# Level 2 cross attention: scores with the keys on the partitions, maxima found and spread by two transpositions

## The chip, the cores and the metric

The kernel runs on one core of one Trainium2 chip. The time is that of the device, in microseconds (us), from start to end of one execution; a median of several executions is given where there are several. Everything is computed in fp32.

## The reference, cut to what matters

The reference is a four-level perceiver: each level is a cross attention to a long context, an attention-like mixing of the latent rows, and a feed-forward part. The changed part is the cross attention of level 2. It has 2 batches of 64 latent rows with 256 features, 2 batches of 1024 context rows with 192 features, and 16 heads of 64 features.

```python
def _L2_xattn_ref(x, context, w_q, w_k, w_v, w_o, b_o):
    ...
    q = (x @ w_q).reshape(B, Sq, HEADS, DIM_HEAD).transpose(0, 2, 1, 3)
    k = (context @ w_k).reshape(B, Skv, HEADS, DIM_HEAD).transpose(0, 2, 1, 3)
    v = (context @ w_v).reshape(B, Skv, HEADS, DIM_HEAD).transpose(0, 2, 1, 3)
    sim = jnp.einsum('bhid,bhjd->bhij', q, k) * SCALE
    attn = jax.nn.softmax(sim, axis=-1)
    out = jnp.einsum('bhij,bhjd->bhid', attn, v)
    out = out.transpose(0, 2, 1, 3).reshape(B, Sq, INNER)
    return out @ w_o + b_o
...
x = x + _L2_xattn_ref(_layernorm(x, axis=-1), ctx_768, ...)
```

No mask is applied in this part.

## The kernel before

All 128 latent rows (2 batches of 64) lie on the 128 partitions, and the program goes through the levels one after the other, stage by stage. Each stage opens its own pools of SBUF tiles. Two pools lie in PSUM: `two_banks()` gives a tile of 1024 columns over two banks, `bank()` one of 512; in this stage there are two of the first kind and four of the second, and a tile is given again when its last reader is done. `weight(name)` takes a tile from a ring of weight tiles and issues its load on the SP queue. `stat()` gives a small tile from a ring.

The cross attention of level 2 (L1545 to L1656) never forms keys or values. The query of each head is multiplied with the head's key weights instead, so that scores are products of a 192-wide query with the raw context; the output is the weighted sum of raw context rows, multiplied with the head's value weights afterwards.

1. L1555 to L1564: layernorm of x, its transposition, and the queries of all heads, `qT`, scaled by 0.125. Around it run the last steps of `kv3.values`, work for level 3 that fills waits of PE.
2. L1569 to L1585: queries through the key weights, to `qA` (the first 128 of 192 context features) and `qB` (the other 64, kept twice, once on each half of the partitions), in four groups of eight matmuls; each group fills a `two_banks()` tile and is evicted by `evacuate`, which alternates between VectorE and ScalarE.
3. L1595 to L1651: the loop over 16 units, a unit being a pair of heads `j` and a batch `b`. A unit has 128 queries (2 heads x 64 rows) and 1024 keys. Scores have the queries on the partitions and the keys on the columns: `qA` is the stationary operand and the turned context `ctxA` (128 features) streams by in two pieces of 512 keys (L1601); the 64 remaining features, `ctxB`, are added by two matmuls on the two halves of the array (L1606). VectorE takes the maximum of each query over its 1024 keys (L1611), ScalarE the exponential with the negated maximum as its bias, and the sum of the row with it (L1613).
4. The second part of a unit, `finish`, runs one unit later (`later`, L299): p is turned in eight pieces of 128x128 (`transposed`, L244; PE at L251, copies at L102 and L104), the turned pieces weigh the context rows `crows` (`accumulate`, L261, eight matmuls of 192 columns), and VectorE divides by the row's sum, giving `u` (L1624).
5. The third part, `project`, runs one unit later still: `u` is turned (L1629), copied by ScalarE to `uT` (L1632), and for every second unit multiplied with the value weights (L1641) and copied to `oT` (L1647).
6. L1654 to L1656: the product with `wo` and the residual. The sum of x and the bias is done on GpSimd (`residual`, L263).

An fp32 matmul shows in the profile as two records, each with its weight load, and a transposition as one. Only the layernorm part of the stage stands in `in_written_order` (L273), which ties each instruction of PE, VectorE, ScalarE and GpSimd to the one written before it on the same engine; the order of the rest is found by the scheduler of the language, which is free to bring later scores ahead of weighing.

The context rows `crows` are loaded at L1550 with one DMA of 12288 contiguous bytes per partition. On the SP queue it stands between the loads of level 2's next stage (`l2t_qkv` ahead of it, `l2t_gate`, `l2t_val`, `l2t_proj` behind it).

## Time and profile before

| | |
|---|---|
| median of 3 runs | 725.84 us (725.58 to 725.9) |
| profiled execution: its own time | 727.3 us |
| profiled execution: span of the records | 725.6 us |
| mean granted TensorE clock | 0.976 |
| PE busy, share of the span | 670.8 us, 92% |
| VectorE (DVE) busy | 286.9 us, 40% |
| ScalarE (ACT) busy | 266.6 us, 37% |
| GpSimd (POOL) busy | 65.9 us, 9% |
| level 2 cross attention: first scores to the first matmul with `wo` | 284.72 to 398.45 |

PE is TensorE's matmuls, PEld its weight loads, which overlap them. Times inside the profile are us from the start of the span; "L261" is a line of the kernel file, and a line can be that of a helper (all accumulated matmuls of the program have L261). A row of the timeline gives the start, the length, the engine, the line, the operation, what it writes and reads, and, in brackets, how long the engine sat idle before it and what ended that. A row of the groups gives the busy time of all instructions of one line and form and the mean length of one in nanoseconds. The lengths of matmuls are modelled, and overlapping ones are counted once.

### The profile page before, as it was taken

To read this page: it belongs to the slowest core of one execution; us is meant where nothing else is said; L and a number is where in the kernel's file an instruction comes from. 1 tells how busy PE (TensorE), PEld (TensorE's weight loads), DVE (VectorE), ACT (ScalarE), POOL (GpSimd) and SP (SyncE) were. 2 spreads that over 40 slices of the span, in tenths; PEclk is the share of its full clock that TensorE was granted. 3 is DMA by queue.
4 is the path that set the end of the run, shared out by engine and by line. 5 is a ranking of instruction groups with operands and counts; after the bars stand their busy time and mean duration, and the time that the engine had idled before them with its cause. 6 is when DMAs were issued, how large, how long until landed. Compare 5 with 4: busy or idle time off the path is not lost.

```text
span 725.6 us, 11293 instructions
## 1 busy us (share of the span) xinstructions
PE 670.8 (92%) x4628; PEld 493.7 (68%) x4628; DVE 286.9 (40%) x724; ACT 266.6 (37%) x540; POOL 65.9 (9%) x92
## 2 busy tenths in 40 slices
PE   7799979989989999999999989999999989779997
PEld 3456657946659996767766678999979856543543
DVE  5844443157550003343333335525331267533111
ACT  2353252258643333333323324405231278432111
POOL 3520100000100000000000030130000000000340
PEclk9899999989999999999999999999999999969999
DMA  8940012840007886000000400011138800447981
GB/s 283 412 175 1 1 50 92 291 170 1 3 1 255 305 282 261 1 0 1 1 1 1 174 1 1 1 63 55 59 132 312 304 8 2 157 206 296 361 328 66
DMA packets 19302, 92.76 MB, mean 128 GB/s; under 512 B 3042, under 2 KB 5620, under 8 KB 10324
## 3 DMA queue, kind: packets, MB, share of 16 engines
q1 hardware_dynamic: 16976, 85.70, 31.8%
q0 software_dynamic: 2016, 6.30, 2.3%
q8 instruction: 36, 0.59, 0.3%
q14 instruction: 14, 0.11, 0.0%
q10 hardware_dynamic: 260, 0.06, 0.0%
HBM read 98.20 MB, written 0.13 MB: 136 GB/s over the span
## 4 chain that ended last, share of the span: by engine, by line
PE 85%; DVE 8%; ACT 5%; issue 2%; DMA 0%; POOL 0%; DVEq 0%; ACTq 0%; POOLq 0%
PE bank L261 34%; PE two_banks L590 5%; PE two_banks L1601 4%; PE bank L1343 4%; PE bank L251 3%; PE two_banks L1314 3%; PE bank L635 2%; PE two_banks L1606 2%; PE two_banks L379 2%; PE bank L1369 2%; PE two_banks L1773 2%; PE bank L1893 2%; PE two_banks L405 1%; PE two_banks L381 1%; PE two_banks L261 1%
## 5 line engine op out<-in xcount | busy, mean ns | idle before, releaser
L261 PEld LDWEIGHTS bank<-l2x_ctx,pT 128*128 128x128 f32 x256 | 42.3, 190 | 7.8 <-ACT pT L104 4.7
L261 PE MATMUL bank<-l2x_ctx,pT 128*128 128x192 f32 x256 | 44.4, 327 | 0.6 <-ACT pT L104 0.6
L354 DVE SCALAR_TENSOR_TENSOR x_new<-bank,comb,x_new 128x256 f32<-128x256 f32 x24 | 11.6, 484 | 80.0 <-PE bank L261 80.0
L1343 PEld LDWEIGHTS bank<-ident,p 128*128 128x128 f32 x256 | 29.9, 150 | 18.1 <-issue 6.5
L1343 PE MATMUL bank<-ident,p 128*128 128x128 f32 x256 | 39.8, 300 | 1.3 <-ACT pT L1352 0.5
L1322 DVE TENSOR_REDUCE negmax<-two_banks 128x1 f32<-128x1024 f32 x32 | 37.6, 1216 | 7.0 <-PE two_banks L1314 7.0
L1328 ACT ACTIVATE p<-two_banks,negmax 128x1024 f32<-128x1024 f32 x32 | 36.0, 1126 | 0.8 <-DVE negmax L1322 0.8
L1601 PE MATMUL two_banks<-ctxA,l2x_qA 128*128 128x512 f32 x64 | 32.6, 597 | 0.5 <-DVE l2x_qA L102 0.5
L1352 ACT COPY pT<-bank 128x512 f32<-128x512 f32 x48 | 27.0, 588 | 14.4 <-PE bank L1343 14.3
L1532 ACT ACTIVATE l1f_hT<-bank,cols 128x128 f32<-128x128 f32 x64 | 18.2, 368 | 32.9 <-PE bank L261 32.9
L261 PEld LDWEIGHTS bank<-xT,l1f_w_sb 128*128 128x128 f32 x256 | 29.7, 192 | 0.6 <-issue 0.3
L261 PE MATMUL bank<-xT,l1f_w_sb 128*128 128x128 f32 x256 | 30.1, 276 | 0.0
L261 PEld LDWEIGHTS bank<-xT,l2f_w_sb 128*128 128x128 f32 x256 | 29.6, 192 | 0.3
L261 PE MATMUL bank<-xT,l2f_w_sb 128*128 128x128 f32 x256 | 29.8, 276 | 0.0
L104 ACT COPY pT<-bank 128x512 f32<-128x512 f32 (+1 forms) x22 | 12.1, 556 | 47.6 <-PE bank L251 47.6
L261 PE MATMUL bank<-l1f_w_sb,l1f_hT 128*128 128x256 f32 x128 | 28.8, 380 | 0.0
L1611 DVE TENSOR_REDUCE negmax<-two_banks 128x1 f32<-128x1024 f32 x16 | 19.6, 1225 | 20.8 <-PE two_banks L1606 20.8
L1314 PE MATMUL two_banks<-n_kT,n_qx 32*128 32x512 f32 x128 | 24.7, 667 | 2.8 <-ACT n_kT L450 1.8
L251 PEld LDWEIGHTS bank<-ident,p 128*128 128x128 f32 x164 | 17.7, 141 | 13.8 <-issue 11.8
L261 PEld LDWEIGHTS bank<-l1f_w_sb,l1f_hT 128*128 128x128 f32 x128 | 23.8, 190 | 2.9
L268 POOL TENSOR_TENSOR x_bias<-x_new,rows 128x256 f32<-128x256 f32 x4 | 2.9, 725 | 235.1 <-DVE x_new L354 230.6
L590 PE MATMUL two_banks<-l3f_w_sb,m_xg 128*64 128x512 f32 (+1 forms) x112 | 23.4, 636 | 0.5 <-ACT m_xg L613 0.5
(558 smaller groups left out, 1313.8 us busy)
## 6 DMA issues: line engine op xcount, KB each, us to landing
l1f_w_sb<-in_l1f_w_dram SPq DMA_DIRECT2D x16, 1024.0 KB, 4.9
l3f_w_sb<-in_l3f_w_dram SPq DMA_DIRECT2D x12, 1024.0 KB, 7.5
more_w<-in_l3f_w_dram SPq DMA_DIRECT2D x12, 1024.0 KB, 11.5
l0f_w_sb<-in_l0f_w_dram SPq DMA_DIRECT2D x8, 1024.0 KB, 9.1
l2f_w_sb<-in_l2f_w_dram SPq DMA_DIRECT2D x8, 1024.0 KB, 4.7
l2f_w_sb<-in_l2f_w_dram SPq DMA_DIRECT2D x8, 512.0 KB, 4.5
xh<-in_ctx_dram SPq DMA_DIRECT2D x8, 192.0 KB, 5.8
l2x_ctx<-in_ctx_dram SPq DMA_DIRECT2D x1, 1536.0 KB
```

The lines of the kernel that those rows point to most:

```text
L251: nc.tensor.transpose(ps[:, c * P : (c + 1) * P], src[:, (at + c) * P : (at + c + 1) * P], ident)
L261: nc.tensor.matmul(dst, lhsT, rhs, start=(k == 0), stop=(k == len(pairs) - 1))
L379: nc.tensor.matmul(dst[n], ctxA[:, b, n, keys], w[:, 0, :], start=True, stop=False)
L590: nc.tensor.matmul(part[s], xg[r][:, c, s], shelf.at[r, j, n](c, f), start=False, stop=(c == 1), skip_group_check=True,)
L1314: nc.tensor.matmul(sc[u][:, n * 512 : (n + 1) * 512], qx[rows_, c, n, b].rearrange("p h q -> p (h q)"), kT[c, b][rows_, n, :], start=True, ...
L1322: nc.vector.tensor_reduce(sc[u][1], sc[u][0], AX.X, ALU.max, negate=True)
L1328: nc.scalar.activation(p[u], sc[u][0], AF.Exp, bias=sc[u][1], scale=1.0, accum_out=total[u // 4][:, u % 4 : u % 4 + 1],)
L1343: nc.tensor.transpose(ps[:, kc * P : (kc + 1) * P], p[u][:, (4 * k + kc) * P : (4 * k + kc + 1) * P], ident,)
L1352: nc.scalar.copy(dst, ps)
L1532: nc.scalar.activation(hT[:, at + f, :], ps[:, f * P : (f + 1) * P], AF.Gelu, bias=col("l1f_b1", e * 8 + at + f), scale=1.0,)
L1601: nc.tensor.matmul(dst[n], qA[:, j, b].rearrange("p h q -> p (h q)"), ctxA[:, b, n, :], start=True, stop=False,)
L1611: nc.vector.tensor_reduce(negmax, sc, AX.X, ALU.max, negate=True)
```

## The change

Scores now have the keys on the partitions: for each of eight blocks of 128 keys, the context block is the stationary operand and the unit's 128 queries stream by. The weights p come out turned as weighing needs them, so p is not transposed any more. The maximum of a query now lies across partitions. It is found in two steps: VectorE takes the maximum over the eight blocks (`largest`, a view with a step of 128 elements), PE turns the resulting 128x128 tile (`turn_largest`), VectorE takes the maximum over its columns, negated (`largest_of_all`), and a second transposition, of that column broadcast to 128 columns, spreads the values over the partitions (`spread`), with a copy to SBUF by ScalarE. VectorE then adds the negated maximum to the scores on their way from PSUM to SBUF (`shift`, two halves), and ScalarE takes the exponential in place (`exponentials`, two halves). `crows` gets a 193rd column of ones, so that weighing also yields the sum of the weights. The whole stage stands in `in_written_order`, with an order written out in the loop at its end. The queries are evicted by halves on both engines, `through_keys` uses two single banks where it used a tile of two banks, and its last call is moved behind the first scores. The tiles for attention have two buffers where they had three.

```diff
@@ -1542,115 +1542,179 @@
 
 
 
+
+
     with psum(2, 4), stage_pool(name="l2x", bufs=1) as pool, stage_pool(
-        name="l2x_att", bufs=3
-    ) as att:
+        name="l2x_att", bufs=2
+    ) as att, in_written_order():
         wq, wk, wv, wo = (weight(f"l2x_w{n}") for n in "qkvo")
-        crows = pool.tile([P, 16, CD], F32, name="l2x_ctx")
-        nc.sync.dma_start(crows, i["ctx"])
-        with in_written_order():
-
-            last = kv3.values(1, 2)
-            steps(last, 2)
-            xlT = turned_rows(layernorm(x, then=AF.Exp))
-            steps(last)
+
+        crows = pool.tile([P, 16, CD + 1], F32, name="l2x_ctx")
+        nc.sync.dma_start(crows[:, :, :CD], i["ctx"])
+        nc.gpsimd.memset(crows[:, :, CD:], 1.0)
         qT = pool.tile([P, 8, P], F32, name="l2x_qT")
-        for at in (0, 4):
+
+
+        qA = pool.tile([P, 8, NB, 2, S], F32, name="l2x_qA")
+        qB = pool.tile([P, 8, NB, 2, S], F32, name="l2x_qB")
+        oT = pool.tile([P, 8, P], F32, name="l2x_oT")
+        units = [(j, b) for j in range(8) for b in range(NB)]
+        sc, mx, turned_mx, shifts, p, po, u, uT = {}, {}, {}, {}, {}, {}, {}, {}
+
+        def queries(at):
             ps = features(xlT, wq, at, 4)
             dst = qT[:, at : at + 4, :].rearrange("p c t -> p (c t)")
-            if at == 0:
-                nc.vector.tensor_scalar(dst, ps, 0.125, None, ALU.mult)
-            else:
-                nc.scalar.activation(dst, ps, AF.Copy, scale=0.125)
-
-
-        qA = pool.tile([P, 8, NB, 2, S], F32, name="l2x_qA")
-        qB = pool.tile([P, 8, NB, 2, S], F32, name="l2x_qB")
-        for at in (0, 4):
-            for part, qc in enumerate((qA, qB)):
-                ps = two_banks()
-                for j in range(4):
-                    for h in range(2):
-                        nc.tensor.matmul(
-                            ps[:, h * 512 + j * P : h * 512 + (j + 1) * P],
-                            wk[half[h], at + j, part * P : (part + 1) * P],
-                            qT[half[h], at + j, :], start=True, stop=True,
-                        )
+            nc.vector.tensor_scalar(dst[:, :D], ps[:, :D], 0.125, None, ALU.mult)
+            nc.scalar.activation(dst[:, D:], ps[:, D:], AF.Copy, scale=0.125)
+
+        def through_keys(at, part):
+            ps = [bank(), bank()]
+            for j in range(4):
                 for h in range(2):
-                    evacuate(
-                        qc[:, at : at + 4, :, h, :],
-                        ps[:, h * 512 : (h + 1) * 512].rearrange(
-                            "p (j b q) -> p j b q", j=4, b=NB
-                        ),
+                    nc.tensor.matmul(
+                        ps[h][:, j * P : (j + 1) * P],
+                        wk[half[h], at + j, part * P : (part + 1) * P],
+                        qT[half[h], at + j, :], start=True, stop=True,
                     )
-        oT = pool.tile([P, 8, P], F32, name="l2x_oT")
-        outer = []
-
-        def last_part(work=None):
-            if outer:
-                outer.pop()()
-            if work is not None:
-                outer.append(work)
-
-        for j in range(8):
-            uT = att.tile([CH, 2, 2, NB, S], F32, name="l2x_uT", bufs=2)
-            for b in range(NB):
-                sc = two_banks()
-                dst = [sc[:, n * 512 : (n + 1) * 512] for n in range(2)]
+            for h, copy in enumerate((nc.vector.tensor_copy, nc.scalar.copy)):
+                copy(
+                    (qB if part else qA)[:, at : at + 4, :, h, :],
+                    ps[h].rearrange("p (j b q) -> p j b q", j=4, b=NB),
+                )
+
+        def scores(k):
+
+            j, b = units[k]
+            sc[k] = two_banks().rearrange("p (n t q) -> p n t q", n=2, t=4)
+            for n in range(2):
+                for t in range(4):
+                    nc.tensor.matmul(
+                        sc[k][:, n, t, :], ctxA[:, b, n, t * P : (t + 1) * P],
+                        qA[:, j, b].rearrange("p h q -> p (h q)"),
+                        start=(t == 0), stop=False, skip_group_check=True,
+                    )
+            for t in range(4):
                 for n in range(2):
                     nc.tensor.matmul(
-                        dst[n], qA[:, j, b].rearrange("p h q -> p (h q)"), ctxA[:, b, n, :],
-                        start=True, stop=False,
+                        sc[k][:, n, t, :], ctxB[half[n], b, t * P : (t + 1) * P],
+                        qB[half[n], j, b].rearrange("p h q -> p (h q)"),
+                        start=False, stop=True, skip_group_check=True,
                     )
-                for n in range(2):
+
+        def largest(k):
+            mx[k] = att.tile([P, P], F32, tag="mx", name="l2x_mx")
+            nc.vector.tensor_reduce(
+                mx[k], sc[k].rearrange("p n t q -> p q (n t)"), AX.X, ALU.max
+            )
+
+        def turn_largest(k):
+            turned_mx[k] = bank()
+            nc.tensor.transpose(turned_mx[k][:, :P], mx[k], ident)
+
+        def largest_of_all(k):
+            mx[k] = stat(name="negmax")
+            nc.vector.tensor_reduce(mx[k], turned_mx[k][:, :P], AX.X, ALU.max, negate=True)
+
+        def spread(k):
+
+            ps = turned_mx[k][:, P : 2 * P]
+            nc.tensor.transpose(ps, mx[k].to_broadcast([P, P]), ident)
+            shifts[k] = att.tile([P, P], F32, tag="shift", name="l2x_shift")
+            nc.scalar.copy(shifts[k], ps)
+
+        def shift(k):
+            p[k] = att.tile([P, 2, 4, P], F32, tag="p", name="p")
+            for n in range(2):
+                nc.vector.tensor_tensor(
+                    p[k][:, n], sc[k][:, n], shifts[k].unsqueeze(1).to_broadcast([P, 4, P]),
+                    ALU.add,
+                )
+
+        def exponentials(k):
+            for n in range(2):
+                nc.scalar.activation(p[k][:, n], p[k][:, n], AF.Exp)
+
+        def weigh(k, kcs):
+            _, b = units[k]
+            if kcs[0] == 0:
+                po[k] = bank()
+            for kc in kcs:
+                nc.tensor.matmul(
+                    po[k][:, : CD + 1], p[k][:, kc // 4, kc % 4, :], crows[:, b * 8 + kc, :],
+                    start=(kc == 0), stop=(kc == 7),
+                )
+
+        def take_u(k):
+            rinv = stat(name="rinv")
+            nc.vector.reciprocal(rinv, po[k][:, CD : CD + 1])
+            u[k] = att.tile([P, CD], F32, tag="u", name="l2x_u")
+            nc.vector.tensor_scalar(u[k], po[k][:, :CD], rinv, None, ALU.mult)
+
+        def turn_u(k):
+            j, b = units[k]
+            if b == 0:
+                uT[j] = att.tile([CH, 2, 2, NB, S], F32, tag="uT", name="l2x_uT")
+            ps = bank()
+            for c in range(2):
+                nc.tensor.transpose(
+                    ps[0:CH, c * P : (c + 1) * P], u[k][:, c * CH : (c + 1) * CH], ident
+                )
+            nc.scalar.copy(
+                uT[j][:, :, :, b, :],
+                ps[0:CH, : 2 * P].rearrange("p (c h q) -> p c h q", c=2, h=2),
+            )
+
+        def project(k):
+            j, b = units[k]
+            if b == 0:
+                return
+            ps = bank()
+            for c in range(2):
+                for h in range(2):
                     nc.tensor.matmul(
-                        dst[n], qB[half[n], j, b].rearrange("p h q -> p (h q)"),
-                        ctxB[half[n], b, :], start=False, stop=True,
+                        ps[half[h], :P],
+                        wv[:, c, (2 * j + h) * 64 : (2 * j + h + 1) * 64],
+                        uT[j][:, c, h].rearrange("p b q -> p (b q)"),
+                        start=(c == 0), stop=(c == 1),
                     )
-                negmax, total = stat(name="negmax"), stat(name="total")
-                nc.vector.tensor_reduce(negmax, sc, AX.X, ALU.max, negate=True)
-                p = att.tile([P, NK], F32, tag="p", name="p")
-                nc.scalar.activation(p, sc, AF.Exp, bias=negmax, scale=1.0, accum_out=total)
-                rinv = stat(name="rinv")
-                nc.vector.reciprocal(rinv, total)
-
-                def finish(j=j, b=b, p=p, rinv=rinv, uT=uT):
-                    pT = transposed(p, 8, att, "pT", "pT")
-                    po = bank()
-                    accumulate(
-                        po[:, :CD], [(pT[:, kc, :], crows[:, b * 8 + kc, :]) for kc in range(8)]
-                    )
-                    u = att.tile([P, CD], F32, name="l2x_u")
-                    nc.vector.tensor_scalar(u, po[:, :CD], rinv, None, ALU.mult)
-
-                    def project():
-                        ps = bank()
-                        for k in range(2):
-                            nc.tensor.transpose(
-                                ps[0:CH, k * P : (k + 1) * P], u[:, k * CH : (k + 1) * CH], ident
-                            )
-                        nc.scalar.copy(
-                            uT[:, :, :, b, :],
-                            ps[0:CH, : 2 * P].rearrange("p (k h q) -> p k h q", k=2, h=2),
-                        )
-                        if b == 0:
-                            return
-                        ps = bank()
-                        for k in range(2):
-                            for h in range(2):
-                                nc.tensor.matmul(
-                                    ps[half[h], :P],
-                                    wv[:, k, (2 * j + h) * 64 : (2 * j + h + 1) * 64],
-                                    uT[:, k, h].rearrange("p b q -> p (b q)"),
-                                    start=(k == 0), stop=(k == 1),
-                                )
-                        nc.vector.tensor_copy(oT[:, j, :], ps[:, :P])
-
-                    last_part(project)
-
-                later(finish)
-        later()
-        last_part()
+            nc.vector.tensor_copy(oT[:, j, :], ps[:, :P])
+
+
+        last = kv3.values(1, 2)
+        steps(last, 2)
+        xlT = turned_rows(layernorm(x, then=AF.Exp))
+        steps(last)
+        queries(0)
+        queries(4)
+        through_keys(0, 0)
+        through_keys(0, 1)
+        through_keys(4, 0)
+        for k in range(-1, 16):
+            if k < 15:
+                scores(k + 1)
+                largest(k + 1)
+            if k > 0:
+                turn_u(k - 1)
+            if k >= 0:
+                weigh(k, range(0, 4))
+            else:
+                through_keys(4, 1)
+            if k < 15:
+                turn_largest(k + 1)
+                largest_of_all(k + 1)
+            if k >= 0:
+                weigh(k, range(4, 6))
+            if k < 15:
+                spread(k + 1)
+                shift(k + 1)
+                exponentials(k + 1)
+            if k >= 0:
+                weigh(k, range(6, 8))
+                take_u(k)
+            if k > 0:
+                project(k - 1)
+        turn_u(15)
+        project(15)
         ps = bank()
         accumulate(ps[:, :D], [(oT[:, k, :], wo[:, k, :]) for k in range(8)])
         x = residual(x, ps[:, :D], row("l2x_bo"))
```

## Prediction

> **What bounds the kernel now.** I read the page first, then the windows of the stage, then the timeline of one unit, then the groups for single durations. The page's first part and two windows (columns: length, then busy time and count of PE, PEld, DVE, ACT, POOL, then the granted clock, the DMA share and GB/s):
>
> ```profile
> PE 670.8 (92%) x4628; PEld 493.7 (68%) x4628; DVE 286.9 (40%) x724; ACT 266.6 (37%) x540; POOL 65.9 (9%) x92
> ...
> 305.00:385.00 80.00, 80.00 (x443) 56.17 (x442) 29.33 (x54) 25.00 (x47) 0.25 (x1) 1.00 0.00 1
> 385.00:398.00 13.00, 11.21 (x70) 8.34 (x70) 3.88 (x8) 3.96 (x9) 0.57 (x4) 1.00 0.00 0
> ```
>
> In the body of this stage PE is never idle, at full clock and with nothing on the DMA engines; DVE and ACT work about a third of the time. So here time is the sum of what PE streams, and only PE's list of work counts, until some wait opens a hole in it. One unit (head pair j, batch b) in the timeline (start, length, engine, line):
>
> ```profile
> 342.96 0.38 PE L1629 MATMUL bank<-ident,l2x_u 128*96 128x128 f32 x2
> ...
> 343.18 1.02 PE L1601 MATMUL two_banks<-ctxA,l2x_qA 128*128 128x512 f32 x2
> ...
> 344.13 1.13 PE L1606 MATMUL two_banks<-ctxB,l2x_qB 64*128 64x512 f32 x4
> ...
> 345.19 1.09 PE L251 MATMUL bank<-ident,p 128*128 128x128 f32 x8
> 345.31 1.23 DVE L1611 TENSOR_REDUCE negmax<-two_banks 128x1 f32<-128x1024 f32 x1 [1.73 <-PE two_banks L1606]
> ...
> 346.12 1.02 PE L1601 MATMUL two_banks<-ctxA,l2x_qA 128*128 128x512 f32 x2
> ...
> 346.98 2.76 PE L261 MATMUL bank<-l2x_ctx,pT 128*128 128x192 f32 x16
> ...
> 349.58 0.38 PE L1629 MATMUL bank<-ident,l2x_u 128*96 128x128 f32 x2
> ```
>
> Matmuls are pipelined, so I count from one start to the next: turning u 0.22, scores over ctxA 0.95 and 0.86, over ctxB 1.06, the eight transpositions of p 0.93, weighing 2.60. That is 6.62; units with the projection add 0.59 (its first start 336.92 to 337.51), so 6.92 on average and 110.6 for 16 units. The stage's own bounds are 284.72 (first scores) and 398.45 (first matmul with wo), 113.7: 3.1 are stalls at its end.
>
> **The change, part by part.**
>
> *Eight transpositions of p and their two copies go.* PE: -0.93 per unit. The copies (DVE 0.68, ACT 0.59) lay beside PE and give nothing.
>
> *Scores with the context stationary.* Over ctxA there are now 16 records of 128 columns with a weight load each, where 4 of 512 stood. The nearest rows are the expert features of level 1, same shape:
>
> ```profile
> 225.96 3.73 PE L261 MATMUL bank<-xT,l1f_w_sb 128*128 128x128 f32 x32
> 229.53 3.62 PE L261 MATMUL bank<-l1f_w_sb,l1f_hT 128*128 128x256 f32 x16
> ```
>
> 3.57/32 = 0.1116 per record, loads hidden. 16 of them are 1.79, with the same 0.09 of change-over 1.88, against 1.81: +0.07. Over ctxB the pairs of 64-row matmuls run side by side as L1606's do now (1.06 is 2 x 0.43 and some 0.2 of change-over): 8 x 0.1116 + 0.2 = 1.09, +0.03. A lower end: L1574 has this very shape and loads 32 weights in 1.86, which would make it 0.9, -0.16. An upper end, loads not hidden at their 0.19 each, is excluded by the features row. I take +0.03.
>
> *Two transpositions per unit for the maxima*: 2 x 0.116 (0.93/8) = +0.23. *The sum of weights as a 193rd column* in weigh: 16 records x 1/192: +0.01.
>
> Sum on PE: -0.93 + 0.07 + 0.03 + 0.23 + 0.01 = -0.59 per unit, **-9.4 for 16**, if no new wait opens.
>
> *The new chain on DVE and ACT.* Per unit: the maximum over eight key blocks (1024 elements), the reduce of the turned maxima (L1017: 0.28), the spread's copy on ACT (L1845: 0.265), two shifts of 128x512 with a PSUM operand (L1811: 0.686 each), two exponentials from SBUF (L1812: 0.63 each), reciprocal 0.16, u 0.42, oT 0.15 on average.
>
> ```profile
> L1611 DVE TENSOR_REDUCE negmax<-two_banks 128x1 f32<-128x1024 f32 x16 | 19.6, 1225 | 20.8 <-PE two_banks L1606 20.8
> ...
> L1811 DVE TENSOR_TENSOR a<-two_banks,a 128x512 f32<-128x512 f32 x2 | 1.3, 686 | 1.3 <-PE two_banks L1790 1.3
> ...
> L1017 DVE TENSOR_REDUCE neg<-bank 128x1 f32<-128x128 f32 x4 | 1.1, 280 | 0.0
> ...
> L498 DVE TENSOR_SCALAR own_e<-iota,pmod 128x512 f32<-128x512 f32 x1 | 0.7, 673 | 0.0
> ```
>
> DVE comes to 3.6 and ACT to 1.9 (0.265 + 1.26 + uT 0.37) of a unit of 6.3: neither is the bound. The order of waits decides. PE waits in order, so everything behind a waiting transposition waits too.
>
> (1) turn_largest waits for the reduce. Now the reduce starts 0.12 after PE's next start (345.19 to 345.31); with 1.225 and 0.07 to reach PE it needs 1.42. Between scores and turn_largest PE has turn_u 0.22 and eight records of weigh 1.30: 1.52. Slack 0.10, and the weight load of the transposition (0.14) can't be pulled ahead: I book 0.05.
> (2) spread waits for transposition 0.27, reduce 0.28, two hops of about 0.05, load 0.14: 0.79; cover 0.12 and four records 0.65: 0.77. I book 0.05. Bounds for both together: 0 to 0.3 per unit; 0.1 x 15 = **+1.5**.
> (3) weigh of the next unit waits for shifts and exponentials: about 2.1 after spread for the first half, 2.8 for the second; PE has at least 0.65 + 2.97 + 0.22 before it. Hidden, with over 1 us to spare; without that cover it would be 2 per unit.
> (4) take_u now stands behind the shifts on DVE, 2.7 after spread, and turn_u comes 3.7 after. Hidden, but not in the last unit, where there are no scores.
>
> *The reduce is the open price.* It reads PSUM with a step of 128 elements, and the trace of before has no reduce over such a view. Row: L498 writes SBUF with a step of 64 elements, 673 ns for 512, what a contiguous copy of 512 takes (L102: 684). The rule against it: the Trainium skill, Vector Engine (DVE) Microarchitecture Reference, section Measured stream behaviour on trn2, says that a port runs at full rate only on adjacent pairs of words, and gives 1.73 ns per column for one source that hops at each element, against 1.054, and 1.71 for a hopping output. On L498 it would make an estimated 0.34 more than measured; so this trace disagrees for a write. The page measured SBUF, not PSUM. By the row the reduce is 1.225. By the rule it is an estimated 1.225 + 1024 x 0.68 ns = 1.92, (1) becomes a wait of 0.59, 9.4 in all, and the change would end 0.7 slower. I take the row, because its measured instruction runs on this chip in this kernel, and keep both ends.
>
> *Start and end.* Queries are evicted by halves and through_keys uses four single banks, so its 0.5 us stalls at 282.15 and 284.72 go; first scores at about 282.45. But the fourth through_keys (0.95) moves behind scores(0), and the first unit shows its chain bare: turn_largest(0) stands 0.5, spread(0) 0.9, since the DVE copy of the moved through_keys (0.69) is ahead of the reduce. 282.45 + 0.95 + 1.4 = 284.8: equal to now. End: turn_u(14) waits 1.3 for take_u behind the shifts, then 0.95 and 0.7 around u(15): 3.0, against 3.1. Zero for both.
>
> *Queues.* SP: the ctx load keeps its place (issued 271.80, after the level 1 experts' last matmuls) but lands in rows of 768 bytes with a gap. Its landing isn't shown; l2t_gate, issued 0.4 later behind it, lands after 8.4, so ctx is in by 281. First weigh now comes at about 291: 10 us cover it, and a load at half the speed still fits. The loads behind it (gate, val, proj) are first used after 410. l2t_projT, which waits for the last use of wv, moves with the stage. POOL: a memset of 16 elements per partition, ahead of x_bias, which isn't needed before 402; POOL is idle. Orders pinned on all four engines: no instruction added.
>
> **Sum**: -9.4 + 1.5 = -7.9. The profiled execution took 727.3 with a span of 725.6, so 1.7 around it; its span would be 717.7. The median of the runs shown, 725.84, is 1.5 below that execution; from it: **717.9**.
>
> **The rivals.**
> *Strided reduce.* One mechanism, one place: DVE's maximum over the view with step 128, PE waiting at turn_largest. It decides from where the waits eat 9.4 - 0.8: 0.54 per unit, a reduce of about 1.87. For: the rule above. Against: L498. At the rule's price 726.5; at 2.5 ns per element (which the same table gives for small hops) the reduce is about 2.7, the wait 1.4, and the time 739.
> *More gain.* ctxB's pairs at L1574's rate and no waits: 3 + 1.5 more, 713.4. For: same shape. Against: 0.2 of change-over stands in L1606 today.
> *Thin cover.* Each of the four hops per unit costs 0.1 more than read: 0.3 to 0.4 per unit in place of 0.1, 721.5 to 722.5. For: slack is 0.1 and less. Against: hops measured at 0.05 to 0.07.
> That the transpositions were hidden anyway would make the change worth nothing; PE's 80.00 busy of 80.00 excludes it.
>
> **How the numbers follow.** Forecast (715.5 to 720.5) 0.47; more gain 0.13; thin cover 0.12; strided reduce near the rule's price (724 to 729) 0.19, of which 0.03 faster, 0.06 within, 0.10 slower; dearer than that 0.09. 0.2%, about what a measurement of this kernel can tell, is 1.45 us. Faster 0.75, same 0.06, slower 0.19. 713.5 to 727.5 leaves out the dearest reduces and little below. Without the reduce's case: 714 to 722.
>
> **What would show it.** Right: no transposition of p, 1.2 us for the maximum, one unit in 6.3 to 6.5, PE idle under 2 us between 290 and 380, most of it before the transpositions of the maxima. Wrong: the maximum at 1.8 or more, with as much PE idle before turn_largest; ctxA's scores over 1.9; PE waiting for ctx; or any stall in the stages behind that was not there.

## The result and the profile after

The changed kernel took 720.45 us (median of 4 runs, 718.91 to 721.7) where the kernel before took 725.87 in the same series. The ratio is 0.9915, with a 95% interval of 0.9892 to 0.9939. A second, larger series, in the run "again" below, gave 0.9899 (0.9879 to 0.9919). So the change gains 5 to 7 us. The forecast of 717.9 was 2.5 too low against the first median, which lies just inside the likeliest range (715.5 to 720.5), at its upper edge. The profiled execution took 721.7, with a span of 719.9.

The page after, its first part. PE has more instructions than before and less busy time; VectorE has gained the shifts and the second reduce, and lost the copies of the turned p:

```profile
PE 663.7 (92%) x4916; PEld 514.3 (71%) x4916; DVE 300.7 (42%) x757; ACT 262.4 (36%) x541; POOL 65.6 (9%) x93
```

The windows of the stage's body and end (length; busy time and count of PE, PEld, DVE, ACT, POOL; granted clock, DMA share, GB/s):

```profile
290.00:380.00 90.00, 90.00 (x777) 83.50 (x778) 47.11 (x89) 25.98 (x56) 0.00 (x0) 1.00 0.03 12
380.00:393.00 13.00, 10.63 (x89) 9.27 (x87) 5.61 (x13) 4.39 (x9) 0.30 (x1) 1.00 0.00 0
```

PE is still busy without a hole for the whole body: the bound has not changed, only PE's list has become shorter. One unit of the timeline, with a projection (343.98 to 350.85), and the end of the one before it:

```profile
340.35 0.82 PE L1642 MATMUL bank<-l2x_ctx,p 128*128 128x193 f32 x4
341.01 1.95 PE L1591 MATMUL two_banks<-l2x_qA,ctxA 128*128 128x128 f32 x16
342.89 1.16 PE L1598 MATMUL two_banks<-l2x_qB,ctxB 64*128 64x128 f32 x16
343.98 0.42 PE L1659 MATMUL bank<-ident,l2x_u 128*96 128x128 f32 x2
344.10 1.23 DVE L1606 TENSOR_REDUCE l2x_mx<-two_banks 128x128 f32<-128x1024 f32 x1 [1.37 <-PE two_banks L1598]
...
344.24 1.48 PE L1642 MATMUL bank<-l2x_ctx,p 128*128 128x193 f32 x8
...
345.40 0.14 PEld L1612 LDWEIGHTS bank<-ident,l2x_mx 128*128 128x128 f32 x1
345.56 0.27 PE L1612 MATMUL bank<-ident,l2x_mx 128*128 128x128 f32 x1
...
345.67 0.82 PE L1642 MATMUL bank<-l2x_ctx,p 128*128 128x193 f32 x4
345.87 0.29 DVE L1616 TENSOR_REDUCE negmax<-bank 128x1 f32<-128x128 f32 x1 [0.54 <-PE bank L1612]
...
346.32 0.27 PE L1621 MATMUL bank<-ident,negmax 128*128 128x128 f32 x1
...
346.43 0.82 PE L1642 MATMUL bank<-l2x_ctx,p 128*128 128x193 f32 x4
...
347.18 0.66 PE L1674 MATMUL bank<-l2x_uT,l2x_wv_sb 96*64 96x128 f32 x8
...
347.77 2.05 PE L1591 MATMUL two_banks<-l2x_qA,ctxA 128*128 128x128 f32 x16
...
349.75 1.16 PE L1598 MATMUL two_banks<-l2x_qB,ctxB 64*128 64x128 f32 x16
...
350.85 0.42 PE L1659 MATMUL bank<-ident,l2x_u 128*96 128x128 f32 x2
```

Counted from start to start, this unit takes 6.87; the next one, without a projection, ends at 356.93, after 6.08. The mean of the two kinds is 6.475 where the kernel before had 6.92: 0.44 less, 7.1 for 16 units. The reduce with its step of 128 in PSUM takes 1.23, ends at 345.33, and the weight load that needs it starts at 345.40, still beside the weighing: turn_largest does not wait.

From the first matmul with wq to the first with wo, the stage went from 122.64 (275.81 to 398.45) to 115.15 (277.91 to 393.06): 7.5 less. Behind it nothing got slower: from the first matmul with wo to the end of the span it is 326.8, and 327.2 in the kernel before. But the stage began 2.1 later in this profile. The run "again" shows where such a delay comes from.

### The profile page after: what moved, and what is told of

Same layout as the page of the kernel before. It is cut to its first block, busy times and chain, and to the rows that moved or that the text cites. A ratio compares the mean times of both kernels' runs of the same rounds, so it can differ in the third digit from the quotient of the medians.

```text
span 719.9 us, 11877 instructions
## 1 busy us (share of the span) xinstructions
PE 663.7 (92%) x4916; PEld 514.3 (71%) x4916; DVE 300.7 (42%) x757; ACT 262.4 (36%) x541; POOL 65.6 (9%) x93
## 4 chain that ended last, share of the span: by engine, by line
PE 84%; DVE 9%; ACT 4%; issue 2%; DMA 0%; POOL 0%; DVEq 0%; ACTq 0%; POOLq 0%
PE bank L261 29%; PE bank L1642 6%; PE two_banks L590 5%; PE two_banks L1591 4%; PE bank L1343 4%; PE two_banks L1314 3%; PE bank L635 3%; PE two_banks L1598 2%; PE bank L1369 2%; PE two_banks L1837 2%; PE bank L1957 2%; PE two_banks L405 1%; PE two_banks L379 1%; PE two_banks L261 1%; PE bank L1945 1%
## 5 line engine op out<-in xcount | busy, mean ns | idle before, releaser
L1642 PE MATMUL bank<-l2x_ctx,p 128*128 128x193 f32 x256 | 48.1, 327 | 0.0
L354 DVE SCALAR_TENSOR_TENSOR x_new<-bank,comb,x_new 128x256 f32<-128x256 f32 x24 | 11.6, 484 | 79.7 <-PE bank L261 79.7
L1343 PEld LDWEIGHTS bank<-ident,p 128*128 128x128 f32 x256 | 29.9, 150 | 18.5 <-issue 7.8
L1642 PEld LDWEIGHTS bank<-l2x_ctx,p 128*128 128x128 f32 x256 | 40.8, 191 | 0.4
L1322 DVE TENSOR_REDUCE negmax<-two_banks 128x1 f32<-128x1024 f32 x32 | 37.6, 1216 | 7.2 <-PE two_banks L1314 7.2
L1591 PE MATMUL two_banks<-l2x_qA,ctxA 128*128 128x128 f32 x256 | 31.9, 278 | 0.0
L261 PEld LDWEIGHTS bank<-xT,l1f_w_sb 128*128 128x128 f32 x256 | 31.3, 201 | 0.6 <-issue 0.3
L1591 PEld LDWEIGHTS two_banks<-l2x_qA,ctxA 128*128 128x128 f32 x256 | 30.3, 192 | 1.1 <-issue 1.0
L1606 DVE TENSOR_REDUCE l2x_mx<-two_banks 128x128 f32<-128x1024 f32 x16 | 19.6, 1225 | 26.5 <-PE two_banks L1598 26.5
L1628 DVE TENSOR_TENSOR p<-two_banks,l2x_shift 128x512 f32<-128x512 f32 x32 | 20.6, 687 | 13.1 <-ACT l2x_shift L1623 13.1
L1635 ACT ACTIVATE p<-p 128x512 f32<-128x512 f32 x32 | 19.6, 630 | 12.1 <-DVE p L1628 12.1
```

The source lines that it names most:

```text
L261: nc.tensor.matmul(dst, lhsT, rhs, start=(k == 0), stop=(k == len(pairs) - 1))
L1322: nc.vector.tensor_reduce(sc[u][1], sc[u][0], AX.X, ALU.max, negate=True)
L1343: nc.tensor.transpose(ps[:, kc * P : (kc + 1) * P], p[u][:, (4 * k + kc) * P : (4 * k + kc + 1) * P], ident,)
L1591: nc.tensor.matmul(sc[k][:, n, t, :], ctxA[:, b, n, t * P : (t + 1) * P], qA[:, j, b].rearrange("p h q -> p (h q)"), start=(t == 0), stop= ...
L1606: nc.vector.tensor_reduce(mx[k], sc[k].rearrange("p n t q -> p q (n t)"), AX.X, ALU.max)
L1628: nc.vector.tensor_tensor(p[k][:, n], sc[k][:, n], shifts[k].unsqueeze(1).to_broadcast([P, 4, P]), ALU.add,)
```

## The experiments

All stage lengths below are from the first matmul with wq to the first with wo. The changed kernel's two profiles give 115.15 both times, while its single times differ by 2 and more; so the stage's length in one profile tells a difference of some tenths.

**again**: no edit.

> The changed kernel once more. In its first profile the level 2 cross attention, from the first matmul with wq to the first with wo, took 115.15 where the kernel before took 122.64 (7.5 less), but the stages ahead of it began it 2.1 later. Theory: those 2.1 are the granted clock and its phase, which changes from run to run; then the stage again takes 115.1 to 115.3, the start of the stage moves by 1 to 2 either way, and the time is 718 to 720.5. Rival: the change itself costs 2 in the stages ahead; then the stage begins at 277.5 to 278.2 again and the time is 720 to 722.

It took 719.12 (5 runs, 717.4 to 721.06), and the stage took 115.15 again. The stage began at 277.6. The experts of level 1, ahead of the stage, last from one layernorm to the next: 211.21 to 274.39 in the first profile, 63.2, and 212.55 to 274.10 in this one, 61.5; the kernel before has 61.5. Here are eight microseconds of them in the first profile, then the same eight, counted from the first layernorm, in this one:

```profile
214.00:218.00 4.00, 4.00 (x22) 4.00 (x23) 1.57 (x11) 0.81 (x2) 0.00 (x0) 0.57 0.00 0
218.00:222.00 4.00, 3.63 (x28) 3.01 (x28) 0.70 (x2) 2.29 (x8) 0.00 (x0) 1.00 0.21 55
```

```profile
215.34:219.34 4.00, 4.00 (x36) 4.00 (x37) 1.57 (x11) 1.95 (x6) 0.00 (x0) 1.00 0.00 0
219.34:223.34 4.00, 3.63 (x29) 3.01 (x28) 0.70 (x2) 1.76 (x7) 0.00 (x0) 1.00 0.68 227
```

In the first profile four microseconds ran at a mean granted clock of 0.57 with PE busy all the time, 22 matmul records in place of 36; in the second the same work ran at 1.00. Four microseconds at 0.57 are 4 x 0.43 = 1.7 lost, which is the 1.6 between the two lengths. It comes and goes: of the ten profiles, all with the same work in that stage, four have 63.2 (this first one, "price", "order" and "head") and six 61.5, the kernel before among them.

This run's own stage was late as well, by 1.8, though its experts of level 1 took 61.5. Its dip lies further ahead, in level 0. First the kernel before, then this run:

```profile
108.00:116.00 8.00, 6.25 (x30) 4.11 (x30) 3.93 (x12) 1.98 (x4) 0.00 (x0) 1.00 0.21 69
```

```profile
108.00:116.00 8.00, 7.22 (x21) 4.93 (x22) 2.95 (x8) 0.59 (x2) 0.00 (x0) 0.57 0.20 69
```

Between two instructions on either side of it, L1215 and the first L354 behind that, lie 21.10 in the kernel before (101.25 to 122.35) and 23.60 here (100.87 to 124.47): 2.5 more. So in both profiles a dip of the clock that the profile before does not have at that place accounts for most of the delay, and nothing points to a cost of the change ahead of its stage. The start of this run's stage was inside the range that was written down for the rival, so that mark alone would not have told the two apart. The places of the dips do, and so do the starts in the later variants of the changed kernel (274.7 to 277.0, on both sides of the 275.8 of the kernel before).

**price**: the maximum made about as long as the rule that the prediction weighed would have it.

```diff
             mx[k] = att.tile([P, P], F32, tag="mx", name="l2x_mx")
+            nc.vector.tensor_reduce(
+                stat(name="more"), sc[k][:, 0].rearrange("p t q -> p (t q)"), AX.X, ALU.max
+            )
             nc.vector.tensor_reduce(
```

> The changed kernel with one more maximum, over 128x512 elements (0.69), on VectorE ahead of each unit's own maximum; its result is not used. It gives the maximum the length that the strided reduce would have had by the rule that was weighed in the prediction. Theory: turn_largest has no slack to speak of (in the profile after, the reduce ends 0.07 before the weight load, which just fits), so nearly all of the 0.69 shows on PE: 0.6 to 0.67 per unit, 9.5 to 10.7 in all, time 729 to 731, slower than the kernel before. Rival: PE or the order has slack that the reading misses; then under 4 more, 720 to 724.

It took 728.97 (5 runs), a ratio of 1.0042 (1.0022 to 1.0063) to the kernel before: slower than it. The stage took 123.4, 8.3 more than the changed kernel's and 0.8 more than before. The waits of PE between 290 and 380, and the places in the timeline:

```profile
PE bank L1615 <- DVE l2x_mx L1609: 4.0, 13, 0.5
```

```profile
346.39 0.69 DVE L1606 TENSOR_REDUCE more<-two_banks 128x1 f32<-128x512 f32 x1 [1.37 <-PE two_banks L1598]
346.53 1.48 PE L1645 MATMUL bank<-l2x_ctx,p 128*128 128x193 f32 x8
347.00 1.21 DVE L1609 TENSOR_REDUCE l2x_mx<-two_banks 128x128 f32<-128x1024 f32 x1
348.27 0.14 PEld L1615 LDWEIGHTS bank<-ident,l2x_mx 128*128 128x128 f32 x1 [0.55 <-DVE l2x_mx L1609]
348.27 0.33 PE L1615 MATMUL bank<-ident,l2x_mx 128*128 128x128 f32 x1 [0.26 <-DVE l2x_mx L1609]
```

The second maximum starts 0.61 after the first (346.39 to 347.00), not 0.69, so this kernel stands for a maximum of about 1.225 + 0.61 = 1.83. From the weighing's start to turn_largest it is 1.74 (346.53 to 348.27) where the changed kernel has 1.32 (344.24 to 345.56): 0.42 of the 0.61 shows. In the other half of the units it is 1.83, and 0.51 shows. So 0.1 to 0.2 are covered: that is the true slack, not nil as I had written. With a slower restart behind it a unit is 0.47 to 0.54 longer, 8.3 in all. Once the load of the transposition waits, its matmul starts with it (0 to 0.03 later), and the load's 0.14 is not paid on top. The idle 0.26 of the wait line is less than what is lost, because matmuls' ends are modelled; starts tell it.

**nomax**: the maximum left out.

```diff
-            for n in range(2):
-                nc.vector.tensor_tensor(
-                    p[k][:, n], sc[k][:, n], shifts[k].unsqueeze(1).to_broadcast([P, 4, P]),
-                    ALU.add,
-                )
...
-                nc.scalar.activation(p[k][:, n], p[k][:, n], AF.Exp)
+                nc.scalar.activation(p[k][:, n], sc[k][:, n], AF.Exp)
...
-                largest(k + 1)
...
-                turn_largest(k + 1)
-                largest_of_all(k + 1)
...
-                spread(k + 1)
-                shift(k + 1)
```

> The changed kernel without the maximum: no reduces, no two transpositions, no spread, no shift; ScalarE takes the exponential of the raw scores from PSUM in two halves. It leaves out the subtraction of the maximum (and with it the guard against overflow). Theory: PE is the bound and the waits inside the loop are nil, so it gains the two transpositions of 16 units (0.11 each, 3.5), the two bare waits at the start (0.43 and 0.46) and most of the wait of 1.1 at the end: 5 to 5.7 less than the changed kernel, 713.5 to 715.5. Rival: the chain through VectorE and ScalarE still holds PE back in the loop; then 8 or more less, 712 or below. Third: the time hangs on something else, and under 3 are gained.

It took 715.82 (4 runs, 713.76 to 717.71), its stage 109.5: 5.6 less than the changed kernel's. Its units are 5.86 and 6.64, each 0.22 less, which is the two transpositions: 3.6 in 16 units. The two bare waits at the start (0.9) and most of the wait of 1.1 at the end make up the rest. So inside the loop the chain through VectorE and ScalarE costs PE nothing. The body's window:

```profile
291.00:380.00 89.00, 89.00 (x763) 83.23 (x764) 9.81 (x34) 19.98 (x44) 0.00 (x0) 1.00 0.02 6
```

VectorE's load drops from 47.11 of 90 to 9.81 of 89, without any further gain.

**n192**: the column of ones left out, and with it the sum of the weights, so the output is not that of the layer.

```diff
-        crows = pool.tile([P, 16, CD + 1], F32, name="l2x_ctx")
-        nc.sync.dma_start(crows[:, :, :CD], i["ctx"])
-        nc.gpsimd.memset(crows[:, :, CD:], 1.0)
+        crows = pool.tile([P, 16, CD], F32, name="l2x_ctx")
+        nc.sync.dma_start(crows, i["ctx"])
...
-                    po[k][:, : CD + 1], p[k][:, kc // 4, kc % 4, :], crows[:, b * 8 + kc, :],
+                    po[k][:, :CD], p[k][:, kc // 4, kc % 4, :], crows[:, b * 8 + kc, :],
...
-            nc.vector.reciprocal(rinv, po[k][:, CD : CD + 1])
+            nc.vector.reciprocal(rinv, po[k][:, :1])
```

> The changed kernel without the column of ones: the context rows lie without gaps, so the DMA writes 12288 contiguous bytes per partition again, weighing has 192 columns, no memset; u is divided by a column of the weighted sum in place of the sum of the weights, so its values are left out. Theory: 0.2 less at most (16 records of 193 columns a unit are 0.01 longer than of 192), since the load is covered. Rival: the odd width, the gaps or the load in rows of 768 bytes cost PE or delay first weighing; then 1 or more less than the changed kernel.

719.25 (5 runs) against 719.12 for the changed kernel in the same series; stage 114.7 against 115.15. The time shows no difference, the stage 0.4, more than the 0.2 expected and less than the rival's 1. A unit without a projection is 6.06 (348.16 to 354.22) against 6.08, which over 16 units is those 0.4: they are the width. The load of 768-byte rows with gaps delays nothing, and first weighing does not wait in either.

**head**: one part alone, in the kernel before: the changed kernel's `queries` and `through_keys`, in written order.

```diff
-        for at in (0, 4):
-            ps = features(xlT, wq, at, 4)
-            ...
-                ps = two_banks()
+        with in_written_order():
+            queries(0)
+            queries(4)
+            for at in (0, 4):
+                for part in range(2):
+                    through_keys(at, part)
```

> The kernel before with one part of the change alone: queries evicted by halves, through_keys on single banks with its copies on both engines, in written order; all four calls of it before the first scores, and everything behind as before. Theory: the two waits for a copy (0.52 each) go, so scores begin 7.75 after wq and not 8.9, and the rest follows: stage 121.5, time 1.1 less than the kernel before. The orientation of the scores and the transpositions then carry the rest, over 6. Rival: the first unit waits for its exponential anyway and takes it back; then the stage is 122.6.

The stage took 121.4, 1.2 less than the kernel before, with first scores 7.7 after wq (274.72 to 282.41). The time does not show it: 726.09 against 726.3, a ratio of 0.9994 (0.998 to 1.0008) over 22 runs. By the profile 1.2 of the change's 7.5 could be had by the head alone; by the times nothing is proved. The mean granted clock of these 22 executions was 0.9747, that of the kernel before in the same series 0.9761; over 725 us that is an estimated 1.0 lost, if PE was busy in all of it, and would hide the gain. That it did so is not shown. In the change itself most of this is spent again: see below.

**order**: the changed kernel with three pieces moved on PE.

```diff
-                scores(k + 1)
+                scores_a(k + 1, (1,) if k == 0 else (0, 1))
+            if k > 1:
+                project(k - 2)
+            if k < 15:
+                scores_b(k + 1)
...
+            if k == 15:
+                weigh(k, range(0, 4))
...
+            else:
+                scores_a(1, (0,))
...
-            if k > 0:
-                project(k - 1)
```

> The changed kernel with another order on PE: the projection moves between the scores over ctxA and over ctxB of the next unit, where it stood before the change; in the first unit half of the second unit's scores stand ahead of spread; at the end half of the last weighing stands ahead of turn_u(14). Theory: PE's list and its waits are all that count, so a unit with a projection loses the 0.1 to 0.19 by which it is now longer than the sum of its parts (0.8 to 1.5 in all), the first spread's wait of 0.46 goes, and about 0.5 of the 1.1 before turn_u(14): the stage 112.6 to 113.5 where the changed kernel has 115.2, a time 2 below it. Rival: the changes of tile shape cost the same wherever they stand; then only 1 is gained, 114.2.

716.9 (6 runs), ratio 0.9864 (0.9833 to 0.9895) to the kernel before; stage 112.8, 2.4 less than the changed kernel's. The projection stands between the scores over ctxA and over ctxB; the first half of unit 1's scores stands ahead of the first spread, and the last unit's first weighing ahead of the turn of the u before it. A unit of its timeline:

```profile
352.23 0.42 PE L1663 MATMUL bank<-ident,l2x_u 128*96 128x128 f32 x2
...
355.34 1.95 PE L1592 MATMUL two_banks<-l2x_qA,ctxA 128*128 128x128 f32 x16
357.21 0.66 PE L1678 MATMUL bank<-l2x_uT,l2x_wv_sb 96*64 96x128 f32 x8
357.80 1.16 PE L1602 MATMUL two_banks<-l2x_qB,ctxB 64*128 64x128 f32 x16
358.89 0.42 PE L1663 MATMUL bank<-ident,l2x_u 128*96 128x128 f32 x2
```

A unit with a projection is 6.66 here (352.23 to 358.89) and 6.87 in the changed kernel; units without it are 6.08 in both. In the changed kernel the last four weighing records take 0.75 up to the projection (346.43 to 347.18; 0.66 elsewhere), and the scores behind it 1.98 (347.77 to 349.75; 1.88 elsewhere). Between the scores over ctxA and over ctxB, where tile shapes change anyway (128 rows to 64), neither is paid. That the place costs this much is shown; that it is the change of tile shape is my reading of it. One rival can be excluded: the profile after has the projection's weight load start behind the spread's copy on ScalarE, but "nomax" has no such copy, and its units with a projection are longer by the same 0.78 (6.64 and 5.86). Six units with a projection lie whole between scores; they give 1.2 of the 2.4. Another 0.7 comes from the start, where the first spread's wait of 0.46 is gone, and 0.5 from the end. The intervals of this kernel's ratio and of "again" overlap, so it is the profile that shows the gain.

**order_nomax**: both.

> The order of the run called order, without the maximum (it leaves out the subtraction of the maximum, and the guard against overflow with it). Theory: the gains of the two add up but for the waits that are gone in both: the stage 108.2 to 108.9 where the kernel without the maximum has 109.6, the time 1 below that one. Rival: without the spacing that the maxima give, PE waits for the exponentials on ScalarE; then 109.6 or more.

712.37 (6 runs), ratio 0.9789 (0.9763 to 0.9816), stage 108.1, 7.0 less than the changed kernel's. Alone the two had 5.6 and 2.4; the gains add up but for about 1, the waits at the start and the end that both remove. PE waits only 0.8 and 0.5 at the very end. It is the fastest kernel here, at the price of a softmax that nothing keeps from overflowing; with the guard, "order" is the fastest.

**views**: the disputed step by itself, in one unit.

```diff
+            flat = p[k].rearrange("p n t q -> p (n t q)")
+            nc.vector.tensor_reduce(few, p[k].rearrange("p n t q -> p q (n t)"), AX.X, ALU.max)
+            nc.vector.tensor_reduce(few, flat.rearrange("p (q e) -> p q e", e=8), AX.X, ALU.max)
+            nc.vector.tensor_reduce(
+                few, sc[k + 1].rearrange("p n t q -> p (n t q)").rearrange("p (q e) -> p q e", e=8),
+                AX.X, ALU.max,
+            )
+            nc.vector.tensor_copy(many.rearrange("p (e q) -> p q e", e=8), flat.rearrange("p (q e) -> p q e", e=8))
+            nc.vector.tensor_copy(many.rearrange("p (q e) -> p q e", e=8), p[k].rearrange("p n t q -> p q (n t)"))
+            nc.vector.tensor_copy(many, flat)
+            nc.scalar.copy(many.rearrange("p (q e) -> p q e", e=8), p[k].rearrange("p n t q -> p q (n t)"))
+            nc.scalar.copy(many, flat)
```

> The changed kernel, and in one unit, behind take_u on VectorE, six instructions more on other views (their results are not used), and two on ScalarE: (1) maximum over eight blocks of p in SBUF with a step of 128 elements, (2) the same shape without a step in SBUF, (3) without a step in PSUM, (4) a copy of 1024 elements to SBUF writing with a step of 128, (5) reading with that step, (6) without; then (5) and (6) on ScalarE. By the rule of the skill for SBUF: (1) about 1.9, (4) and (5) clearly over (6), by some 0.68 ns per element. By the row of the profile before that had a stepped output: all steps free, (1) = (2) = (3) = 1.22. If (1) is 1.9 and the maximum over PSUM is 1.225, then the price lies in SBUF alone.

Each instruction's length (ns: minimum, median, maximum), in the order of the diff:

```profile
L1687 DVE TENSOR_REDUCE v_few<-p x1: 1908/1908/1908, 326.7 to 326.7; 128x128 f32<-128x1024 f32 x1
L1688 DVE TENSOR_REDUCE v_few<-p x1: 1221/1221/1221, 328.6 to 328.6; 128x128 f32<-128x1024 f32 x1
L1689 DVE TENSOR_REDUCE v_few<-two_banks x1: 1224/1224/1224, 329.9 to 329.9; 128x128 f32<-128x1024 f32 x1
```

```profile
L1693 DVE COPY v_many<-p x1: 1257/1257/1257, 331.0 to 331.0; 128x1024 f32<-128x1024 f32 x1
L1694 DVE COPY v_many<-p x1: 1259/1259/1259, 332.3 to 332.3; 128x1024 f32<-128x1024 f32 x1
L1695 DVE COPY v_many<-p x1: 694/694/694, 333.6 to 333.6; 128x1024 f32<-128x1024 f32 x1
L1696 ACT COPY v_many<-p x1: 1928/1928/1928, 334.4 to 334.4; 128x1024 f32<-128x1024 f32 x1
L1697 ACT COPY v_many<-p x1: 1045/1045/1045, 336.3 to 336.3; 128x1024 f32<-128x1024 f32 x1
```

The maximum with the step takes 1.908 out of SBUF and 1.225 out of PSUM (L1606 in the profile after); without the step 1.22 out of either. So the step costs 0.687, or 0.67 ns per element, in SBUF, and nothing in PSUM. A VectorE copy in SBUF pays for a step on either side, 0.55 ns per element, less than the 0.68 expected. Each instruction here was measured once. This kernel ran once, 726.4 with the profile; its time says only that eight instructions stood on one unit's chain.

## Why the prediction was right, and where its sum was off

*The mechanism*: right. PE's list shortened, no chain took its place, and the saving is found in this stage alone: 7.5 where 7.9 was forecast. That the sum came so close is in part luck, as the next three points show: it counted 2.3 too much on PE's list, and missed 1.5 at the waits and 0.4 at the start and end, which nearly cancel.

*PE's sum per unit*: forecast -0.59, measured -0.44. The parts that were priced by a row came out as priced: ctxA 1.88 (341.01 to 342.89), ctxB 1.09, the two transpositions 0.11 each, weighing 1.32 + 0.65 + 0.66 = 2.63 against 2.61. What failed is a term that was not in the sum. The projection was carried over at 0.59 although it moved, on PE, from between the scores to a place between weighing and scores. In the kernel before:

```profile
335.97 1.02 PE L1601 MATMUL two_banks<-ctxA,l2x_qA 128*128 128x512 f32 x2
336.92 0.66 PE L1641 MATMUL bank<-l2x_uT,l2x_wv_sb 96*64 96x128 f32 x8
337.51 1.13 PE L1606 MATMUL two_banks<-ctxB,l2x_qB 64*128 64x512 f32 x4
```

At its new place it costs 0.19 more, as "order" shows, 0.1 per unit on average. One sign of being wrong came with it: behind a projection ctxA's scores take 1.98, over the 1.9 that the prediction named. u's transpositions take 0.26 and not 0.22; why is open. Asking of a moved step what stands next to it, before and after, would have brought up the first.

*Waits (1) and (2)*: booked at +1.5, measured as none. The window 290 to 380 is all PE. "price" shows a slack of 0.1 to 0.2 before turn_largest, where I had reckoned 0.10 and then added the weight load; the profile after has that load start 0.07 behind the reduce, beside the last weighing.

*The strided reduce*: 1.225 as forecast, but for a reason that the row I chose does not give. L498 is a write, and the copy that I set beside it reads PSUM:

```profile
L102 DVE COPY pT<-bank 128x512 f32<-128x512 f32 x20 | 13.7, 684 | 4.5 <-PE bank L251 4.5
```

In "views" a VectorE copy from SBUF to SBUF takes 694 for 1024 elements without a step and 1257 with one on what it writes. So the 684 for 512 is not what a contiguous write in SBUF takes, and whether L498 paid for its step stays open; it was evidence for neither side. Out of SBUF "views" finds for a maximum what the Trainium skill states (Vector Engine (DVE) Microarchitecture Reference, Measured stream behaviour on trn2): 0.67 ns more per element, against the 0.68 between its 1.73 and 1.054. Out of PSUM the step costs nothing here; that section gives no figure for PSUM. So the forecast of 1.225 came out by luck, not by the row. The price that I set on the rival was nearly right: forecast 0.7 slower than before at 1.92, with a break-even of about 1.87. Measured is a stage 0.8 longer than before's at about 1.83; with 0.05 less per unit it would break even, so I estimate that at 1.78.

*Start and end*: forecast zero. First scores came 6.8 after wq (forecast 6.6), the moved through_keys and waits of 0.43 and 0.46 follow (forecast 0.5 and 0.9), and the end's waits are 1.11, 0.81 and 0.46 (forecast 1.3, 0.95, 0.7):

```profile
289.18 0.33 PE L1612 MATMUL bank<-ident,l2x_mx 128*128 128x128 f32 x1 [0.43 <-DVE l2x_mx L1606]
289.97 0.32 PE L1621 MATMUL bank<-ident,negmax 128*128 128x128 f32 x1 [0.46 <-DVE negmax L1616]
...
387.79 0.40 PE L1659 MATMUL bank<-ident,l2x_u 128*96 128x128 f32 x2 [1.11 <-DVE l2x_u L1651]
391.62 0.40 PE L1659 MATMUL bank<-ident,l2x_u 128*96 128x128 f32 x2 [0.81 <-DVE l2x_u L1651]
392.47 0.66 PE L1674 MATMUL bank<-l2x_uT,l2x_wv_sb 96*64 96x128 f32 x8 [0.46 <-ACT l2x_uT L1662]
```

Together they are 0.4 better than before, the rest of the 7.5. "head" alone gives 1.2, so about 0.8 of that is given back at the start, where the first chain stands bare, and at the end.

*Queues*: as forecast. The memset took 0.12 at 273.94, x_bias followed at 274.44, and the ctx load held nothing up ("n192").

*The time*: 717.9 forecast, 720.45 and 719.12 measured. The first profile began the stage 2.1 later, 1.6 of it from the dip of the clock in the experts of level 1. All four executions of that series had a mean granted clock of 0.974 to 0.976; where in the program it was low is known of the profiled one alone. In the second series the difference of the times is 7.2 (726.31 to 719.12), beside the stage's 7.5.

## What to carry to other kernels

On a stage in which one engine is never idle, write its list of work from start to start, price each line by a row of the same shape, and then check each new wait against what stands before it: a chain of six steps over three engines cost nothing here because each of its waits had a piece of weighing or scores in front of it, the tightest with 0.1 to 0.2 to spare. When a step moves on the bound engine, look at its neighbours, since the same projection cost 0.2 more between two groups of full tiles than at a place where the tile shape changed anyway. And take the price of a strided view from a row of the same kind, a read or a write, in the same memory, or measure it: here the same read was free in PSUM and took half as long again in SBUF.

## What the runs showed of the hardware beyond what was expected

VectorE's maximum reads PSUM with a step of 128 elements as fast as without (1.225 and 1.224 for 1024 elements), but SBUF with the same step at 1.908 where it takes 1.221 without. VectorE's copy in SBUF slows from 0.694 to 1.257 with the step on what it writes and to 1.259 with it on the source, and ScalarE's from 1.045 to 1.928 with it on the source. And a mean granted clock of 0.57, over 4 us in which PE was busy throughout, came in one execution of a program and not in another, worth 1.6 us; a second one, 0.57 over 8 us, was worth 2.5. That is as much as a small change brings: lengths of the changed stage are the better measure where the whole time moves by less.
